# Four-layer block: weight loads moved behind the first expert unit, row one-hots on another engine, and a longer lead of the keys

## The chip, the core and the metric

The kernel runs on one core of a Trainium2 chip. The metric is the device time of one execution in microseconds (us); lower is better. A core has five engines that run their own instruction streams side by side and wait for one another through semaphores: TensorE (PE, matrix products and transpositions), VectorE (DVE), ScalarE (ACT), GpSimd (POOL) and SyncE (SP). SP issues most plain transfers, POOL issues the indirect ones (gathers of rows by an index), and ACT can issue plain transfers too. Each engine works strictly in the order of its own stream.

## What is computed

The input is 32 x 64 x 512 numbers, that is 2048 tokens of 512. Four layers are added to it one after the other, each a "cond" step and an "ffn" step:

```python
x = x + L0_ffn(L0_cond(x))   # per-sample 64x64 mixing; then attention and a
                             # mixture of 7 experts (top 2) with one shared expert
x = x + L1_ffn(L1_cond(x))   # per-sample 64x64 mixing; then 32 experts, top 4
x = x + L2_ffn(L2_cond(x))   # low-rank adapters; then a soft mixture of 16 experts
x = x + L3_ffn(L3_cond(x))   # attention over a paged cache, 8 heads, 4 key groups,
                             # window 256; then a linear layer with int8 weights
```

For layer 1 the router takes the four largest of 32 logits for each token; each token's row goes through its four experts, and the results are added with softmax weights. In layer 3, keys and queries are normalised and rotated per head, the new keys and values are written over the cached ones, and each query attends to the last 256 positions:

```python
q, k, v = x @ Wq.T, x @ Wk.T, x @ Wv.T
q, k = rope(rms(q), pos), rope(rms(k), pos)
k_blocks = k_blocks.at[blk, :, off, :].set(k)      # v likewise
p = softmax(where(in_window, q @ k_all.T * scale, -inf))
out = (p @ v_all) @ Wo.T
```

## The kernel before, in words

Tokens lie in 16 tiles of 128 (NT = 16). The kernel is written in a tile framework: the source says what is done, and a scheduler puts the instructions of each engine in order and inserts the waits. `keep_in_program_order`, `g.pin` and `later=True` hold single instructions to the order of the source. Pools with a number of buffers (`bufs`) decide how far a producer can run ahead.

**Expert layers (class `Moe`).** Tokens are marked in groups of tiles. `put` turns the chosen experts of a group into slots: it makes one-hots over experts, counts with two matmuls (L778, L779) and gets, for each token and choice, a slot number. `mark` then writes token numbers into slots by a matmul of two one-hots: `b_` says which of 128 rows a slot is (L744, 128 wide), `a_` says which tile of slots (L744, 40 tiles wide in layer 1), and ScalarE scales `a_` by the token number (L750). TensorE multiplies them (L752) and VectorE adds the result to `tokens` (L753). Both `a_` and `b_` have one buffer. In layer 1 the groups are `{3: 4, 7: 4, 11: 4, 13: 2, 14: 1, 15: 1}`: three groups of four tiles (n = 4), one of two, two of one. When the last group is marked, `tokens` is copied to the integer `stok` (L792), and by it POOL gathers the rows of the first five slot tiles (`rows_of`, tile `xr`, issued at L284).

Before a tile of layer 1 can be routed, its rows of layer 0's experts are gathered (`yk`) and added to the stream by VectorE (L1010); TensorE applies the per-sample mixing (`mm`, L1094), ScalarE copies it (`c`, L1096), TensorE transposes (`tp`, L1100), ScalarE copies (`cT`, L1102), TensorE multiplies with the router (`rp`, L1105), and VectorE adds the bias (`lg`, L1107) and takes the largest values.

The experts themselves run in units of 320 slots (`run`). Five transposed tiles (`tp`, L924, copied to `xT`) make two units; `into` multiplies with gate and up weights (`gu`, L943), `out_of` with the down weights (`y`, L962). A layer-0 expert has 640 slots (two units), a layer-1 expert 320 (one unit). Weights come as one transfer of 1.5 MB for each expert into a pool of three buffers (`weights`, tile `wt`, issued by SP at L213); the first two are fetched before the experts start, and `run`, which both layers share, asks for the others:

```python
for e in range(3):
    if (u * UNIT // C + e) < E:
        self.weights(u * UNIT // C + e) if u >= 1 or e < 2 else None
```

With `u = 0` the third is not asked for, so the source asks for it in the second unit. It needs nothing but a free buffer, and SP's stream has it early: it is issued at 411.24 us in layer 0, beside the gathers of the first rows, and at 721.83 in layer 1. Beside layer 0's experts, a generator prepares layer 3: it loads constants (`cst3`, `kvlen`, the block table) and the int8 layer's weights `w_i8` (1 MB), computes block numbers on VectorE, and much later reduces `w_i8` to scales (`wsc`).

**Layer 3.** Projections go unit by unit: `kv_i` (keys and values of tile i) and `q_i` alternate, with the queries `LAG` tiles behind (`units`). A unit is four matmuls (`pp`, L1870). For a unit, ScalarE squares (`sq`, L1965), VectorE sums (`ss`), POOL takes the power (`r`, L1970), VectorE normalises (`n`), POOL and VectorE multiply with the rotation tables (`ts` on POOL, `tc` on VectorE, L1988), and VectorE adds (`qkv`, L1997). For keys the tile is written to `newkv`; for queries `heads` transposes it (L1844) into `qT`. Queries from tile `NT - LAG` on are "late": they are copied to `qlate`, and rotated beside the attention by the generator `queries`. The last three tiles' queries (`LAST = 3`) are projected by `project` (L1928) inside the attention loop, at `s = -3, -2, -1`. When all keys are written, POOL gathers the new rows over the cached ones (`new_rows`, tile `kvt`, 96 gathers, L284); the attention loop runs over 64 half-samples: `keys` transposes (`kp`, L2021; copied to `kT`, L2025), `scores` (`sp`, L2048; softmax at L2055 to L2062), `turn` transposes the probabilities (`pT`, L2070), `values` (`op`, L2095), then the output projection (`y`, L2117).

Of the kernel before, what the change touches and what calls it, by code (L numbers as in the profile page):

```python
# [14 lines left out]
AF = mybir.ActivationFunctionType  # L15
ALU = mybir.AluOpType
# [4 lines left out]
P = 128  # L21
B, T, D = 32, 64, 512
NT = B * T // P
# [7 lines left out]
UNIT = 320  # L31
# [367 lines left out]
class Front:  # L399
# [43 lines left out]
    def weights(self, i):  # L443

        self.asked = self.g.cond_weights(self.sb, "wc0", self.at, i) if i < NT else None
# [235 lines left out]
class Moe:  # L681
# [25 lines left out]
        self.wp = ctx.enter_context(tc.tile_pool(name=f"ew{E}", bufs=3, reuse_waits="tile"))  # L707
        self.wts, self.bds = {}, {}

    def weights(self, e):  # L710
        if e < self.E and e not in self.wts:
            t = self.wp.tile([P, self.wlen], F32, name="wt")
            self.g.dma(t, self.g.a[self.wname][e * P : (e + 1) * P, :])
            self.wts[e] = t
        return self.wts.get(e)

# [13 lines left out]
    def mark(self, sb, ps, tok, sl, slot, ov, i, n, tiles):  # L730


        nc, iota, K = self.g.nc, self.g.c("iota"), self.K
        ai = sb.tile([P, n, K], I32, name=f"ai{n}")
        nc.vector.tensor_single_scalar(ai, slot, 7, ALU.arith_shift_right)
        tl = sb.tile([P, n, K], F32, name=f"tl{n}")
        nc.vector.tensor_copy(tl, ai)
        row = sb.tile([P, n, K], F32, name=f"row{n}")
        nc.vector.scalar_tensor_tensor(row, tl, -float(P), sl, ALU.mult, ALU.add)
        nc.vector.tensor_tensor(tl, tl, ov, ALU.add)  # L740
        a_ = sb.tile([P, n * K, tiles], F16, name=f"a_{n}", bufs=1)
        b_ = sb.tile([P, n * K, P], F16, name=f"b_{n}", bufs=1)
        for o, w, v in ((a_, tiles, tl), (b_, P, row)):
            nc.vector.tensor_tensor(  # L744
                o, iota[:, 0:w].unsqueeze(1).to_broadcast([P, n * K, w]),
                v.rearrange("p n k -> p (n k)").unsqueeze(2).to_broadcast([P, n * K, w]), ALU.is_equal,
            )
        for j in range(n):
            aj = a_[:, j * K : (j + 1) * K, :]
            nc.scalar.activation(aj, aj, AF.Copy, scale=self.g.c("tok")[:, i + j : i + j + 1])  # L750
        for k in range(n * K):
            nc.tensor.matmul(ps, b_[:, k, :], a_[:, k, :], start=k == 0, stop=k == n * K - 1)  # L752
        nc.vector.tensor_tensor(tok, tok, ps, ALU.add)  # L753
# [156 lines left out]
    def run(self, xs, per_tile):  # L910

        g, nc, tc, E, K, C = self.g, self.g.nc, self.g.tc, self.E, self.K, self.C
        units = E * C // UNIT
        with ExitStack() as ctx:
            sb = ctx.enter_context(tc.tile_pool(name=f"es{E}", bufs=3, reuse_waits="tile"))
            ps = ctx.enter_context(tc.tile_pool(name=f"eps{E}", bufs=2, space=PSUM, reuse_waits="tile"))
            xrs, xTs, hTs = self.xrs, {}, {}

            def turn(p):
                xT = sb.tile([P, 4, 2 * UNIT], F32, name="xT", bufs=2)  # L920
                for j in range(5):
                    tp = ps.tile([P, 4, P], F32, name="tp", tag="tp")
                    for c in range(4):
                        nc.tensor.transpose(tp[:, c, :], xrs[5 * p + j][:, c * P : (c + 1) * P], g.ident)  # L924
                    out = xT[:, :, j * P : (j + 1) * P]
                    if self.scale is None:
                        g.evac(out, tp)
                    else:
                        nc.vector.tensor_tensor(
                            out, tp, self.scale.unsqueeze(2).to_broadcast([P, 4, P]), ALU.mult  # L930
                        )
                xTs[p] = xT

            def into(u):
                wg, wu, _, bias = self.parts(self.weights(u * UNIT // C))
                xT = xTs[u // 2][:, :, (u % 2) * UNIT : (u % 2 + 1) * UNIT]
                hT = sb.tile([P, 2, UNIT], F32, name="hT", bufs=3)
                for ic in range(2):
                    gu = []
                    for wj in (wg, wu):  # L940
                        o = ps.tile([P, UNIT], F32, name="gu", tag="gu", bufs=4)
                        for c in range(4):
                            nc.tensor.matmul(  # L943
                                o, wj[:, c, ic * P : (ic + 1) * P], xT[:, c, :], start=c == 0, stop=c == 3
                            )
                        gu.append(o)
                    self.act(g, sb, hT[:, ic, :], *gu, None if bias is None else bias[:, ic::2])
                hTs[u] = hT

            def out_of(t):  # L950
                y = ps.tile([P, D], F32, name="y", tag="y")
                p, j = t // 5, t % 5

                pieces = {
                    0: [(0, 0, 0, P)], 1: [(0, P, 0, P)], 2: [(0, 2 * P, 0, 64), (1, 0, 64, 64)],
                    3: [(1, 64, 0, P)], 4: [(1, 64 + P, 0, P)],
                }[j]
                for ic in range(2):
                    for u, col, row, n in pieces:
                        u += 2 * p  # L960
                        wd = self.parts(self.weights(u * UNIT // C))[2]
                        nc.tensor.matmul(  # L962
                            y[row : row + n, :], hTs[u][:, ic, col : col + n], wd[:, ic, :],
                            start=ic == 0, stop=ic == 1,
                        )
                yo = sb.tile([P, D], F32, name="yo", bufs=4)
                if self.bias:
                    for u, col, row, n in pieces:
                        r = slice(row, row + n)
                        bd = self.bds[(u + 2 * p) * UNIT // C]  # L970
                        nc.vector.tensor_tensor(yo[r], y[r], bd[r], ALU.add)  # L971
                else:
                    g.evac(yo, y)
                nc.sync.dma_start(out=self.ys[t * P : (t + 1) * P, :], in_=yo)
                per_tile(sb, ps, t)

            pairs = units // 2
            turn(0)
            for u in range(units):
                p = u // 2  # L980
                if u % 2 == 0 and p + 1 < pairs:
                    self.rows_of(p + 1)
                for e in range(3):
                    if (u * UNIT // C + e) < E:
                        self.weights(u * UNIT // C + e) if u >= 1 or e < 2 else None
                into(u)
                self.bias_of(u * UNIT // C)

                if u % 2 == 0 and p > 0:
                    for j in (2, 3, 4):  # L990
                        out_of(5 * (p - 1) + j)
                if u % 2 == 1:
                    out_of(5 * p)
                    out_of(5 * p + 1)
                    if p + 1 < pairs:
                        turn(p + 1)
            for j in (2, 3, 4):
                out_of(5 * (pairs - 1) + j)
            if isinstance(per_tile, Side):
                per_tile.finish()  # L1000
# [577 lines left out]
def layer3_ahead(g, pool, w):  # L1578
# [15 lines left out]
    nc.sync.dma_start(out=ki, in_=a["kvlen"].rearrange("o b -> b o"))  # L1594
    tab = sb.tile([B, NBLK], I32, name="tabi")
    nc.sync.dma_start(out=tab, in_=a["table"])
    wt = g.load(sb, "w_i8")
    yield

    w["ridx"] = ridx = sb.tile([P, NT], I32, name="ridx")  # L1600
# [29 lines left out]
    nc.vector.tensor_scalar(slots[:, 0:KB], iota[0:B, 0:KB], s0p, None, ALU.add)  # L1630
    nc.vector.tensor_scalar(slots[:, KB:], iota[0:B, 0:5], wsp, None, ALU.add)
    blk = sb.tile([B, KB + 5], F32, name="blk")
    yield
    for j in range(KB + 5):
        hot = sb.tile([B, NBLK], F32, name="hot3", bufs=2)
# [44 lines left out]
    later = []  # L1680
# [85 lines left out]
            yield  # L1766


LAG = 5
LAST = 3  # L1770


def layer3(g, w, xs, xb):
# [3 lines left out]
    with ExitStack() as ctx:  # L1777
# [36 lines left out]
        with ExitStack() as c1:  # L1814
# [38 lines left out]
            for u in range(len(units) + 5):  # L1853
# [10 lines left out]
                if u < len(units):  # L1864
# [4 lines left out]
                    for c in range(4):  # L1869
                        nc.tensor.matmul(  # L1870
                            pp, xT[i][:, c, :], (w["w_kv3"] if z else wq)[:, c, :], start=c == 0, stop=c == 3
                        )
                    late = not z and i >= NT - LAG
                    out = wp.tile([P, D], F32, name=f"qlate{i}") if late else sb.tile([P, D], F32, name="qkv3", bufs=6)
                    outs.append(out)
                    if late:
# [60 lines left out]
        for s in range(-3, last + 8):  # L1937
            if s == -3:
                project(NT - LAST)
            if s % 2 == 0:  # L1940

                if s >= 4:
                    for _ in range(3):
                        old_rows()
                new_rows(s // 2 + 4)
            elif s == -3:
                new_rows(2)
            for stage, at in (("keys", s + 3), ("turn0", s), ("scores", s + 2), ("turn1", s)):
                if 0 <= at <= last:
                    getattr(f, stage)(at)  # L1950
            if -3 < s < LAST - 3:
                project(NT - LAST + s + 3)
            f.out()
            if s >= 2 and s % 2 == 0:
                next(beside, None)
            if 0 <= s - 1 <= last:
                f.values(s - 1)
# [222 lines left out]
```

## Time and profile before

| | |
|---|---|
| runs | 2704.36, 2704.14, 2700.83 us; median 2704.14 |
| the profiled execution | 2703.36 us, span 2701.6 us |
| mean granted TensorE clock | 0.97 |
| busy, share of the span | PE 93%, DVE 52%, ACT 27%, POOL 32% |
| DMA | 343.58 MB in the span, mean 127 GB/s |

Where things happen in the trace of before (us from the start of the span):

| stretch | what |
|---|---|
| 0 to 410 | layer 0: mixing, attention, shared expert, routing |
| 410 to 633 | layer 0's experts |
| 633 to 745 | layer 1's mixing and routing |
| 745 to 1231 | layer 1's experts |
| 1231 to 2279 | layer 2 |
| 2279 to 2392 | layer 3's projections |
| 2392 to 2701 | layer 3's attention and the int8 layer |

How to read the lines: a timeline row has its start, its duration, the engine, the line of the kernel, the operation, the tile written and the tiles read, shapes, the number of instructions that were put together, and in brackets the time for which the engine stood idle just before it and what ended that. A row of busy time by stretch has the stretch, its length, the busy time of PE, PEld (weight loads), DVE, ACT and POOL with the number of instructions, then the granted clock (1.00 is full), the DMA engines' busy share and GB/s. A matmul's end is modelled, so a row of several matmuls is better read by its starts.

### The profile page before, as it was taken

The numbers are of one execution on the slowest core, as the hardware profiler recorded it, in microseconds if no ns is written. First come the engines' busy times: TensorE is split into PE (matmuls) and PEld (weight loads), VectorE is DVE, ScalarE is ACT, GpSimd is POOL, SyncE is SP. The second block draws the span as 40 slices with busy tenths as digits, with TensorE's granted clock in tenths as the row PEclk, the third lists the DMA queues.
The fourth block names the chain that finished last, engine by engine and source line by source line (L and its number), as shares of the span: only waits on it lengthen the run. The fifth ranks groups of instructions, "written<-read, shape, count | busy, mean of one in ns | idle before, by whom it ended". The sixth has DMA issues, their size and how long they took to land.

```text
span 2701.6 us, 42326 instructions
## 1 busy us (share of the span) xinstructions
PE 2524.0 (93%) x16508; PEld 1620.7 (60%) x16523; DVE 1417.6 (52%) x3439; ACT 725.6 (27%) x1503; POOL 852.3 (32%) x904
## 2 busy tenths in 40 slices
PE   7999998996699999996999999999999999979998
PEld 5777775563565555564666666666666665435554
DVE  4666655643744444443544445555544431647886
ACT  2444430111311121110222222222222221236664
POOL 2222214623232233213233333333233321563440
PEclk9999989997699999998999999999999999989999
DMA  2333214445656976544122222222222223423441
GB/s 98 131 126 117 88 67 169 161 147 184 222 184 219 343 256 212 209 173 176 52 73 73 81 80 72 72 72 72 72 75 70 92 63 117 158 77 111 135 136 48
DMA packets 136213, 343.58 MB, mean 127 GB/s; under 512 B 24249, under 2 KB 25049, under 8 KB 128704
## 3 DMA queue, kind: packets, MB, share of 16 engines
q1 hardware_dynamic: 100368, 245.84, 26.3%
q0 software_dynamic: 35056, 89.13, 10.9%
q10 hardware_dynamic: 576, 5.77, 0.5%
q8 instruction: 134, 2.20, 0.3%
q14 instruction: 79, 0.65, 0.1%
HBM read 247.10 MB, written 109.58 MB: 132 GB/s over the span
## 4 chain that ended last, share of the span: by engine, by line
PE 41%; DVE 9%; issue 2%; DMA 1%; ACT 1%; POOL 0%; another core or an unknown queue 0%; SPq 0%; ACTq 0%; POOLq 0%; DVEq 0%
PE out L1557 8%; PE lp L1414 7%; PE pp L1870 3%; PE gp L1546 3%; PE zp L1491 3%; PE yp L1359 2%; PE y L2117 2%; PE hp L1523 2%; PE op L2095 2%; PE pT L2070 2%; PE sp L2048 2%; DVE xt L1025 1%; PE ep L1500 1%; DVE inv L1450 1%; PE kp L2021 1%
## 5 line engine op out<-in xcount | busy, mean ns | idle before, releaser
L943 PE MATMUL gu<-xT,wt 128*128 128x320 f32 x1472 | 408.5, 434 | 0.0
L943 PEld LDWEIGHTS gu<-xT,wt 128*128 128x128 f32 x1472 | 278.7, 191 | 123.4 <-issue 16.4
L1557 PE MATMUL out<-sb_w,gT 128*128 128x512 f32 x512 | 233.5, 599 | 10.7 <-DVE nn L1394 6.6
L962 PE MATMUL y<-wt,hT 128*128 128x512 f32 (+1 forms) x552 | 240.2, 608 | 0.2 <-DVE yo L971 0.2
L1414 PEld LDWEIGHTS lp<-xnT,sb_mu 128*128 128x128 f32 x2048 | 234.8, 193 | 9.2 <-issue 6.7
L1414 PE MATMUL lp<-xnT,sb_mu 128*128 128x128 f32 x2048 | 237.8, 276 | 2.1 <-ACT xnT L254 1.3
L1491 PE MATMUL zp<-sb_w,xnT 128*128 128x512 f32 x512 | 228.6, 595 | 5.1 <-DVE z L1493 5.1
L284 POOL DMA_INDIRECT kvst<-kv,gidx x96 | 97.7, 1017 | 271.6 <-DMA oldkv<-kvst 197.5
L1550 DVE COPY gT<-gp 128x512 f32<-128x512 f32 x64 | 44.3, 692 | 248.8 <-PE gp L1546 248.4
L1557 PEld LDWEIGHTS out<-sb_w,gT 128*128 128x128 f32 x512 | 93.3, 190 | 115.7 <-issue 95.2
L1491 PEld LDWEIGHTS zp<-sb_w,xnT 128*128 128x128 f32 x512 | 93.7, 190 | 113.2 <-issue 100.0
L284 POOL DMA_INDIRECT xr<-rows,stok x115 | 110.3, 959 | 153.3 <-PE tp L924 81.8
L284 POOL DMA_INDIRECT kvt<-newkv,oidx x96 | 97.8, 1019 | 135.6 <-DMA kvt<-oldkv 70.8
L962 PEld LDWEIGHTS y<-wt,hT 128*128 128x128 f32 (+1 forms) x552 | 80.5, 172 | 98.5 <-issue 83.2
L677 POOL TENSOR_TENSOR ga<-ga,sg 128x320 f32<-128x320 f32 x64 | 55.2, 862 | 266.2 <-ACT sg L673 262.7
L284 POOL DMA_INDIRECT yk<-ys,slot x96 | 98.3, 1024 | 128.6 <-SPq L823 66.2
L1528 ACT ACTIVATE h<-hp 128x512 f32<-128x512 f32 x128 | 69.5, 594 | 217.0 <-PE hp L1523 216.8
L673 ACT ACTIVATE sg<-ga 128x320 f32<-128x320 f32 x64 | 30.0, 469 | 278.5 <-DVE ga L671 274.7
L924 PEld LDWEIGHTS tp<-sb_cst,xr 128*128 128x128 f32 x460 | 54.8, 149 | 67.4 <-issue 38.4
L1419 DVE TENSOR_TENSOR lT<-lp,cmu 128x512 f32<-128x512 f32 x64 | 43.5, 680 | 94.5 <-PE lp L1414 93.6
L971 DVE TENSOR_TENSOR yo<-y,bd 128x512 f32<-128x512 f32 (+1 forms) x96 | 66.3, 691 | 50.1 <-PE y L962 46.4
L2055 DVE CUSTOM_DVE_ANT_0 s<-sp,mask 128x336 f32<-128x336 f32 x128 | 60.8, 503 | 59.8 <-PE sp L2048 25.1
(380 smaller groups left out, 4565.0 us busy)
## 6 DMA issues: line engine op xcount, KB each, us to landing
wt<-w_e SPq DMA_DIRECT2D x32, 1538.0 KB
ys<-yo SPq DMA_DIRECT2D x115, 256.0 KB
oldkv<-kvst SPq DMA_DIRECT2D x96, 224.0 KB
kvt<-oldkv SPq DMA_DIRECT2D x96, 224.0 KB
ys<-zero SPq DMA_DIRECT2D x10, 2048.0 KB
xt<-x SPq DMA_DIRECT2D x62, 256.0 KB
x<-xt SPq DMA_DIRECT2D x48, 256.0 KB
wt<-w_e SPq DMA_DIRECT2D x7, 1536.0 KB
```

The lines of the kernel that those rows point to most:

```text
L284: ins = self.nc.gpsimd.indirect_dma_start(out=out, out_offset=None, in_=src, in_offset=bass.IndirectOffsetOnAxis(ap=idx, axis=0), **kw)
L677: nc.gpsimd.tensor_tensor(ga, ga, sg, ALU.mult)
L943: nc.tensor.matmul(o, wj[:, c, ic * P : (ic + 1) * P], xT[:, c, :], start=c == 0, stop=c == 3)
L962: nc.tensor.matmul(y[row : row + n, :], hTs[u][:, ic, col : col + n], wd[:, ic, :], start=ic == 0, stop=ic == 1,)
L971: nc.vector.tensor_tensor(yo[r], y[r], bd[r], ALU.add)
L1414: g.first(e + c, nc.tensor.matmul(lp[:, e, :], w["mu"][:, c, (4 * q + e) * P : (4 * q + e + 1) * P], self.xnT[:, c, :], start=c == 0, stop ...
L1491: g.first(c, nc.tensor.matmul(zp, self.xnT[:, c, :], w["w1"][:, c, cols], start=c == 0, stop=c == 3))
L1528: g.pin(nc.scalar.activation(self.hs[q][b], hp[:, b], AF.Gelu))
L1546: g.first(e + b + k, nc.tensor.matmul(gp[r, e, cols], self.hs[q][b][:, e, r], self.lT[q][:, e, cols], start=True, stop=True))
L1557: g.first(e, nc.tensor.matmul(self.out, self.gTs[q][:, e, :], w["w2"][:, 4 * q + e, :], start=q + e == 0, stop=q + e == 6 and q == 3))
L1870: nc.tensor.matmul(pp, xT[i][:, c, :], (w["w_kv3"] if z else wq)[:, c, :], start=c == 0, stop=c == 3)
L2055: nc.vector.tensor_tensor_reduce(p, sps[j], self.masks[2 * i + half], -0.0625, 3.0e38, ALU.add, ALU.min, m)
```

## The change

It has three parts.

1. `weights` takes an engine that issues the transfer. In `run`, the third expert's weights are asked for right after the first unit's `into`, from ScalarE's queue; this holds for layer 0 and layer 1, which share the code. The load of `w_i8` goes two steps further down in the generator that prepares layer 3, and is held to the order of the source there.
2. In `mark`, for groups of four tiles (layer 1's first three groups, twelve tiles), `row` gets the opposite sign, and ScalarE makes `b_`: 16 times the absolute value of (column number minus row) over 128 columns, then one Relu of (1 minus that) over all 2048. `a_` stays on VectorE, and so do `a_` and `b_` of the smaller groups.
3. In layer 3, `LAG` is 8 (was 5), so the queries run eight tiles behind the keys and values; a new `LATE = 5` keeps the same five queries late. `project` makes tiles 13 and 14 at `s = -3` and tile 15 at `s = -2`. The transposed inputs have `LAG + 3` buffers, so 11 (was 8).

```diff
-    def weights(self, e):
+    def weights(self, e, eng=None):
         if e < self.E and e not in self.wts:
             t = self.wp.tile([P, self.wlen], F32, name="wt")
-            self.g.dma(t, self.g.a[self.wname][e * P : (e + 1) * P, :])
+            self.g.dma(t, self.g.a[self.wname][e * P : (e + 1) * P, :], eng)
...
-        nc.vector.scalar_tensor_tensor(row, tl, -float(P), sl, ALU.mult, ALU.add)
+        wide = n == 4
+        sign = -1.0 if wide else 1.0
+        nc.vector.scalar_tensor_tensor(
+            row, tl, -sign * P, sl, ALU.mult, ALU.subtract if wide else ALU.add
+        )
...
-        for o, w, v in ((a_, tiles, tl), (b_, P, row)):
+        if wide:
+            for k in range(n * K):
+                nc.scalar.activation(
+                    b_[:, k, :], iota[:, 0:P], AF.Abs, bias=row.rearrange("p n k -> p (n k)")[:, k : k + 1]
+                )
+            nc.scalar.activation(b_, b_, AF.Relu, bias=self.g.c("ones")[:, 0:1], scale=-1.0)
+        for o, w, v in ((a_, tiles, tl),) if wide else ((a_, tiles, tl), (b_, P, row)):
...
                 for e in range(3):
-                    if (u * UNIT // C + e) < E:
-                        self.weights(u * UNIT // C + e) if u >= 1 or e < 2 else None
+                    self.weights(u * UNIT // C + e) if u >= 1 or e < 2 else None
                 into(u)
+                if u == 0:
+                    self.weights(2, nc.scalar)
...
-    wt = g.load(sb, "w_i8")
     yield
...
     blk = sb.tile([B, KB + 5], F32, name="blk")
+    wt = g.load(sb, "w_i8", later=True)
     yield
...
-LAG = 5
+LAG = 8
+LATE = 5
...
-                    late = not z and i >= NT - LAG
+                    late = not z and i >= NT - LATE
...
             if s == -3:
                 project(NT - LAST)
+                project(NT - LAST + 1)
...
-            if -3 < s < LAST - 3:
-                project(NT - LAST + s + 3)
+            if -3 < s < LAST - 4:
+                project(NT - LAST + s + 4)
```

The scheduler's order after the change, beside the edits themselves: on ScalarE the copies `c` and `cT` of tiles 13, 14 and 15 come after the third group's Abs and Relu (the second group's stand ahead of tile 12's `cT`); on TensorE `mm` of tile 15 comes after tile 13's `rp`; on VectorE tile 15's first `L1010` comes ahead of the second group's `row`; on POOL the first gathers of `kvt` are mixed with `r` and `ts` of queries 7 to 12.

## The prediction

> **What bounds the kernel now.** I read the page's engine table, then the busy time by stretch, then the timelines of the three stages that the change edits.
>
> ```profile
> PE 2524.0 (93%) x16508; PEld 1620.7 (60%) x16523; DVE 1417.6 (52%) x3439; ACT 725.6 (27%) x1503; POOL 852.3 (32%) x904
> ...
> 416.00:418.00 2.00, 0.52 (x3) 0.52 (x4) 0.00 (x0) 0.00 (x0) 1.42 (x2) 0.50 0.96 377
> ...
> 720.00:730.00 10.00, 6.59 (x42) 5.47 (x42) 8.37 (x35) 4.73 (x8) 0.00 (x0) 0.50 0.92 351
> 730.00:740.00 10.00, 1.48 (x11) 1.24 (x12) 3.94 (x20) 1.34 (x4) 2.84 (x3) 0.50 0.64 210
> ...
> 2420.00:2425.00 5.00, 0.24 (x2) 0.00 (x0) 0.01 (x1) 0.59 (x1) 3.91 (x4) 0.50 0.13 31
> ```
>
> TensorE is busy 93% of the span, so an edit counts only where TensorE waits. Each edit aims at one such hole: layer 0's first expert tiles (412 to 425, DMA share 0.96), layer 1's routing (686 to 745), and the start of layer 3's attention (2392 to 2432). The 0.50 is the granted clock.
>
> **A: third expert's and int8 weights later.** The timeline of TensorE:
>
> ```profile
> 412.70 0.63 PE L924 MATMUL tp<-sb_cst,xr 128*128 128x128 f32 x4 [2.47 <-DMA xr<-rows,stok]
> 417.48 1.11 PE L924 MATMUL tp<-sb_cst,xr 128*128 128x128 f32 x4 [4.15 <-DMA xr<-rows,stok]
> 421.22 1.09 PE L924 MATMUL tp<-sb_cst,xr 128*128 128x128 f32 x4 [2.62 <-DMA xr<-rows,stok]
> ...
> 425.30 7.03 PE L943 MATMUL gu<-xT,wt 128*128 128x320 f32 x25
> ```
>
> TensorE waits for gathered rows. GpSimd issues a gather every 1.25 us from 409.16; the first is usable 2.5 us after its issue ended (410.21 to 412.70). The fifth is issued at 414.27 to 415.22, so with free DMA engines it is usable at 417.7; a transposition (1.1) and the DVE copy (0.68) make 419.5 the start of full work, against 425.30: 5.8 us. Two transfers go from this stretch: 1.5 MB of expert 2 (SP, 411.24) and 1 MB of w_i8 (SP, 418.17), 2.5 of some 5 MB that move at 350 to 400 GB/s. The 0.48 MB of constants stays, so I take **-5**; ends: -6.5, and -1 if the gathers' own pace sets the waits. The moved loads are hidden: expert 2 is used in the fifth unit (about 480), 50 us after its new place behind the second sigmoid (431 to 436); w_i8 is first read by a DVE reduction that moves with it. Uncovered, the expert load would cost 1.5 MB at 390 GB/s, 4 us. On ScalarE's queue only an issue of 0.3 to 0.4 us (SP's rows) stands ahead of the next sigmoid.
>
> The same lines move layer 1's third expert behind its second sigmoid (755.00 now), with waits for earlier gathers and GpSimd; the next sigmoid stands behind it. First use is the third unit's matmul at 771.19, 16 us on, against 4 us of load and 3.3 us for five gathers of 0.26 MB: nothing. Layer 1's first gather is issued at 736.41, when today's loads are mostly in: nothing gained.
>
> The Trainium skill (DMA: Bandwidth & Descriptors, "Issuing engines are not separate DMA queues") says that transfers from all engines share the same DMA engines, so another queue only saves issue time. By it, A pays for the delay of the load, not for ScalarE's queue, and a load issued at once on ScalarE would gain nothing; no row here separates the two.
>
> **B: row one-hots on ScalarE.** DVE loses three comparisons of 2.28 us (L744, 128x2048). ScalarE gets, for each of three groups of four tiles, 16 Abs of 128 columns and a Relu of 2048. Its L750 rows with an operand per partition cost 348 ns at 70 columns and 551 at 320, so 395 at 128; four of 320 in 1.92 us are spaced 0.457, 0.094 less than one lasts. An Abs then adds 0.30, sixteen 4.8; the Relu, on the same line, 1.95. With the four scalings (0.46 ahead, 1.4 behind) a group's train is 8.6 us. Ends: 0.16 an Abs (from the 64-column Exp, 257 ns) and a 1.06 Relu (L542, 1024 columns) give 5.5; 0.457 and 2.1 give 11.3.
>
> The place matters more than the sum. ScalarE runs in order, and what stands behind the trains is this:
>
> ```profile
> 704.60 0.17 DVE L739 SCALAR_TENSOR_TENSOR row<-tl,sl 128x16 f32<-128x16 f32 x1
> 704.89 2.28 DVE L744 TENSOR_TENSOR b<-sb_cst,row 128x2048 f16<-128x2048 f32 x1
> 706.10 0.59 ACT L1096 COPY c<-mm 128x512 f32<-128x512 f32 x1 [0.22 <-PE mm L1094]
> 717.26 2.02 PE L1094 MATMUL mm<-xt,wbd 128*128 128x512 f32 x2
> 723.76 0.19 DVE L1107 TENSOR_TENSOR lg<-rp,bc_b_r 128x32 f32<-128x32 f32 x1 [1.23 <-PE rp L1105]
> 734.73 0.43 PE L752 MATMUL tok<-a,b 128*128 128x80 f16 x4 [3.05 <-ACT a L750]
> ```
>
> In the changed order the copies c and cT of tiles 13, 14 and 15 come after group 3's train, and TensorE's mm of tile 15 comes after tile 13's router matmul. DVE has tile 15's first gathered addition ahead of group 2's row: today DVE waits until 703.93 for a gather issued at 697.78; the one needed is issued 1.45 us later, so it lands at about 705.3 and the row is ready at 705.7, no earlier than today's 704.60. Then: train 2 to 714.3; group 3 reuses the one buffer, so it starts when TensorE has read it (1.25), 715.6; train 3 to 724.2; c 0.59, tp 1.1, cT 0.59, rp 1.9, and latencies: mm of tile 15 at about 728.9 against 717.26, 11.6 us late. From there the chain to the last token matmul is today's, except that group 3's marking is already done, some 1.5 us. I take **+10**. Ends: row at 702.3 (all 2.28 saved), trains of 5.5 and full clock give -3; trains of 11.3 give +17.
>
> The clock enters this. The rows 720 to 740 ran at 0.50, though the longest idle stretch that TensorE shows between 708.9 and 730 is 1.97 us; I keep half clock. At full clock the matmuls on the way (tp 1.1 and rp 1.9 of tile 13; mm 2.02, tp 1.12 and rp 1.92 of tile 15) would halve, 4 us less, and B would be +6. The Trainium skill (TensorE: Matmul & The Clock Gate, "HAM oscillation") warns of idle gaps over some 3.4 us. If shorter gaps left the clock full, that +6 would be the term; the rows speak against it.
>
> **C: keys lead by eight tiles.** Three query projections leave the front of the last key projection, 3.87 us each (3.43 and 0.44): it ends 11.6 us earlier, and the first gather of new rows comes at 2382.2 instead of 2393.82. TensorE's total work is unchanged.
>
> ```profile
> 2393.82 1.22 POOL L284 DMA_INDIRECT kvt<-newkv,oidx  x1 [0.85 <-DMA xt<-x2b]
> 2425.32 0.98 POOL L284 DMA_INDIRECT kvt<-newkv,oidx  x1 [0.30 <-issue]
> ...
> 2394.53 0.63 PE L1844 MATMUL tp<-sb_cst,qkv 128*128 128x128 f32 x4 [2.25 <-DVE qkv L1997]
> 2425.73 0.82 PE L2021 MATMUL kp<-sb_cst,kvt 112*128 112x112 f32 x3 [5.50 <-ACT kT L2025]
> 2431.34 1.47 PE L2095 MATMUL op<-pTs,kvt 112*64 112x128 f32 x12
> ```
>
> The 24 gathers take 1.285 us each. Only after the last (2426.3) do the late copies go through, and the first values matmul comes 5.0 us later. In the changed order the gathers are mixed with the rotations of the queries still to come (r 1.64, ts 1.28), one queue. So GpSimd's work is conserved: from 2382.2 it has only some 4.8 us of idle time today (2.1, 1.77, 0.85), and its train can end at 2421.5, not 11.6 earlier. The rotations, waiting behind gathers, also delay the transpositions of queries 7 to 10, which stand ahead of project(13) in TensorE's order: the one idle of 2.25 becomes several, to about 2406. The gap moves more than it closes: values at 2426.5 to 2431. I take **-3**; ends: -11.6, and +4 if the train ends as late as now and the late heads push the keys.
>
> **Sum.** The profiled execution took 2703.36 (span 2701.6 and 1.8 around it), 0.8 below the median of the runs. 2703.36 - 5 + 10 - 3 = 2705.4, on the median's footing 2706. About 0.2%, 5.4 us, is what a measurement of this kernel can tell from no change.
>
> **Rivals.**
> (1) Slower: ScalarE's train is dearer. With B at +17, -5 + 17 - 3 = +9, 2713. It decides from B over 13.4, an Abs of more than 0.41 us in place of 0.30 (two trains on the path). For: 320 columns are spaced 0.457; against: the 70-column row.
> (2) Faster: the keys' lead pays in full. -5 - 11.6, with B at +6 from full clock: -10.6, 2693. For: TensorE idles 15 us in 2392 to 2428; against: one GpSimd queue.
> (3) A does not do what it says: gathers under their own load keep the pace, A is -1, sum +6, 2710. For: the gathers alone move 2.5 MB there; against: the DMA share of 0.96 with three other transfers.
>
> **Chances.** Forecast 0.48 (no change), rival 1 0.17 and rival 3 0.13 (slower, 0.30), rival 2 0.22 (faster). The range 2693 to 2714 takes in the rivals' centres and leaves out about half of rivals 1 and 2.
>
> **What would show it.** A: gu at full pace from 419 to 420. B: the first layer-1 gather at about 741 if A is taken off (736.41 now plus 10, less 5); c of tile 13 behind Abs and Relu. C: first kvt gather 11 to 12 us earlier against the last kv projection, heads gaps before project(13), values 0 to 5 earlier. Wrong: c of tile 13 not waiting for ScalarE, or the values 8 us earlier.

## The result and the profile after

The changed kernel takes 2711.52 us (median of 20 runs, 2703.76 to 2718.70) against 2700.93 for the kernel before (20 runs): ratio 1.0027, 95% interval [1.0018, 1.0037]: 7.3 us slower by that ratio, while the two medians stand 10.6 us apart (a second measurement, e12 below, gives 10.5). Either way the change makes the kernel slower. The forecast of 2706 (no change) missed by 5.5; the range 2693 to 2714 held it. The profiled execution of after took 2711.10, span 2709.3.

The same lines as before, from the page and from the busy time by stretch of after (line numbers behind the edits are 12 to 16 higher than in before):

```profile
PE 2528.1 (93%) x16508; PEld 1623.8 (60%) x16523; DVE 1412.3 (52%) x3436; ACT 743.6 (27%) x1554; POOL 852.1 (31%) x904
```

```profile
416.00:418.00 2.00, 2.00 (x9) 1.53 (x10) 1.03 (x4) 0.00 (x0) 1.39 (x3) 0.50 0.73 202
...
440.00:450.00 10.00, 7.48 (x28) 3.63 (x26) 8.46 (x28) 0.58 (x1) 4.64 (x5) 0.80 0.38 116
450.00:460.00 10.00, 10.00 (x36) 6.99 (x35) 2.16 (x4) 0.87 (x2) 5.88 (x10) 0.86 0.27 79
720.00:730.00 10.00, 4.68 (x30) 3.91 (x30) 0.55 (x4) 8.63 (x19) 0.00 (x0) 0.50 0.14 52
```

The hole at 416 is closed, as A meant; a new one is open at 440 to 460: TensorE stands for 2.5 of ten us and then runs at a lower clock. In before it was busy throughout at full clock there, and VectorE was full beside it:

```profile
430.00:440.00 10.00, 10.00 (x39) 7.05 (x38) 10.00 (x57) 0.87 (x2) 4.01 (x6) 1.00 0.15 51
440.00:450.00 10.00, 10.00 (x41) 5.32 (x40) 10.00 (x32) 1.61 (x3) 2.87 (x3) 1.00 0.21 61
```

At 720 to 730 ScalarE is what is busy in after.

**A in the timeline of TensorE:**

```profile
412.71 0.63 PE L936 MATMUL tp<-sb_cst,xr 128*128 128x128 f32 x4 [2.50 <-DMA xr<-rows,stok]
414.68 0.66 PE L936 MATMUL tp<-sb_cst,xr 128*128 128x128 f32 x4 [1.34 <-DMA xr<-rows,stok]
...
420.64 18.11 PE L955 MATMUL gu<-xT,wt 128*128 128x320 f32 x62
438.58 3.60 PE L974 MATMUL y<-wt,hT 128*128 128x512 f32 x8
...
442.98 1.07 PE L974 MATMUL y<-wt,hT 128*64 128x512 f32 x2
446.57 1.97 PE L936 MATMUL tp<-sb_cst,xr 128*128 128x128 f32 x8 [2.52 <-DVE xT L941]
448.47 1.98 PE L974 MATMUL y<-wt,hT 128*64 128x512 f32 x4
...
451.29 9.56 PE L955 MATMUL gu<-xT,wt 128*128 128x320 f32 x32
```

The rows arrive sooner and `gu` runs at 420.64 instead of 425.30. But the lead melts: 5.6 us at the very first `gu` (417.73 against 423.38), 4.7 at this row, 3.5 at the first `y` (438.58 against 442.13; the `gu` of after run at half clock until 422), and 0.2 at the third unit's `gu` (451.29 against 451.53). In the last step TensorE stood 2.52 us for a copy `xT`, and the transpositions behind it take 1.97 where eight take 1.04 at full clock. VectorE at that time:

```profile
429.20 0.49 DVE L663 SCALAR_TENSOR_TENSOR sg<-gu,sg 128x320 f32<-128x320 f32 x1 [5.29 <-issue]
...
430.75 0.53 DVE L1650 SCALAR_TENSOR_TENSOR hot<-sb_cst,slots,tabf 32x257 f32<-32x257 f32 x1
...
443.37 0.47 DVE L1650 SCALAR_TENSOR_TENSOR hot<-sb_cst,slots,tabf 32x257 f32<-32x257 f32 x1
...
445.83 1.28 DVE L941 TENSOR_TENSOR xT<-tp,sb_ln 128x512 f32<-128x512 f32 x2
```

Between the first and the last `hot` lie 26 look-ups of layer 3's preparation, spaced 0.41 us. They stood in before too (431.58 to 444.82). Now TensorE comes 3.5 us earlier and the look-ups end only 1.0 earlier: VectorE stood 5.29 us ahead of `sg` first, for ScalarE's sigmoid of 428.73.

The look-ups are not the whole difference. In before the copies `xT` came late as well, 2.7 us behind the start of the transpositions (3.8 in after), and TensorE didn't wait for them:

```profile
442.13 3.60 PE L962 MATMUL y<-wt,hT 128*128 128x512 f32 x8
445.56 1.04 PE L924 MATMUL tp<-sb_cst,xr 128*128 128x128 f32 x8
446.53 2.99 PE L962 MATMUL y<-wt,hT 128*64 128x512 f32 x10
449.36 1.04 PE L924 MATMUL tp<-sb_cst,xr 128*128 128x128 f32 x8
...
451.53 8.78 PE L943 MATMUL gu<-xT,wt 128*128 128x320 f32 x32
```

```profile
448.26 1.27 DVE L929 TENSOR_TENSOR xT<-tp,sb_ln 128x512 f32<-128x512 f32 x2
```

Ten `y` matmuls stood between the first transpositions and the next ones (446.53 to 449.36) and covered the wait; in after there are two (442.98). So by these rows the stall takes late copies and TensorE's new order together.

**B in the timelines of ScalarE, TensorE and GpSimd:**

```profile
708.06 4.78 ACT L751 ACTIVATE b<-sb_cst,row 128x128 f16<-128x128 f32 x16 [1.78 <-DVE lg L1121]
...
713.19 1.99 ACT L754 ACTIVATE b<-b,sb_cst 128x2048 f16<-128x2048 f16 x1
...
718.03 4.78 ACT L751 ACTIVATE b<-sb_cst,row 128x128 f16<-128x128 f32 x16 [1.03 <-DVE row L742]
...
726.42 1.04 ACT L1110 COPY c<-mm 128x512 f32<-128x512 f32 x2
...
730.55 2.06 PE L1108 MATMUL mm<-xt,wbd 128*128 128x512 f32 x2
...
749.54 0.94 POOL L284 DMA_INDIRECT xr<-rows,stok  x1 [45.83 <-DVE stok L804]
```

Sixteen Abs take 4.78 us (0.30 each), the Relu 1.99. The copies `c` of tiles 13 and 14 come at 726.42, when the third train is over, `mm` of tile 15 at 730.55 (717.26 in before), the first gather 13.1 later than in before (2.1 of this was there when the stage began: the last gather of layer 0's results is issued at 702.60 against 700.49).

**C in the timelines of GpSimd and TensorE:**

```profile
2393.71 1.39 POOL L284 DMA_INDIRECT kvt<-newkv,oidx  x1 [2.36 <-DMA kvt<-oldkv]
2395.13 1.67 POOL L1986 TENSOR_TENSOR r<-ss,sb_cst 128x8 f32<-128x8 f32 x1
...
2398.05 1.28 POOL L2004 TENSOR_TENSOR ts<-n,tab 128x512 f32<-128x512 f32 x1
...
2435.14 0.98 POOL L284 DMA_INDIRECT kvt<-newkv,oidx  x1 [0.31 <-issue]
...
2408.75 1.09 PE L1859 MATMUL tp<-sb_cst,qkv 128*128 128x128 f32 x4 [6.34 <-DVE qkv L2013]
2414.30 1.09 PE L1859 MATMUL tp<-sb_cst,qkv 128*128 128x128 f32 x4 [4.46 <-DVE qkv L2013]
2418.56 1.09 PE L1859 MATMUL tp<-sb_cst,qkv 128*128 128x128 f32 x4 [3.17 <-DVE qkv L2013]
```

Set against the first projection (11.2 us later than in before), the first gather is 11.3 us earlier, but the 24th only 1.4: `r` and `ts` stand between them. Three query transpositions wait 14 us for those products.

### The profile page after: what moved, and what is told of

Same layout as the page of the kernel before. It is cut to its first block, busy times and chain, and to the rows that moved or that the text cites. A ratio compares the mean times of both kernels' runs of the same rounds, so it can differ in the third digit from the quotient of the medians.

```text
span 2709.3 us, 42377 instructions
## 1 busy us (share of the span) xinstructions
PE 2528.1 (93%) x16508; PEld 1623.8 (60%) x16523; DVE 1412.3 (52%) x3436; ACT 743.6 (27%) x1554; POOL 852.1 (31%) x904
## 4 chain that ended last, share of the span: by engine, by line
PE 41%; DVE 10%; issue 1%; POOL 1%; DMA 1%; ACT 0%; SPq 0%; ACTq 0%; POOLq 0%; DVEq 0%
PE out L1571 8%; PE lp L1428 7%; PE gp L1560 3%; PE pp L1885 3%; PE zp L1505 3%; PE yp L1373 2%; PE y L2133 2%; PE hp L1537 2%; PE op L2111 2%; PE pT L2086 1%; PE sp L2064 1%; DVE xt L1039 1%; PE ep L1514 1%; DVE inv L1464 1%; DVE mx L1441 1%
## 5 line engine op out<-in xcount | busy, mean ns | idle before, releaser
L1571 PE MATMUL out<-sb_w,gT 128*128 128x512 f32 x512 | 233.5, 599 | 11.2 <-DVE nn L1408 6.6
L1466 POOL TENSOR_TENSOR eT<-eT,inv 128x512 f32<-128x512 f32 x64 | 71.8, 1122 | 57.9 <-DVE inv L1465 34.3
```

Of the source, the lines that this page charges most:

```text
L1466: g.pin(nc.gpsimd.tensor_tensor(e3, e3, inv.unsqueeze(2).to_broadcast([P, 8, T]), ALU.mult))
L1571: g.first(e, nc.tensor.matmul(self.out, self.gTs[q][:, e, :], w["w2"][:, 4 * q + e, :], start=q + e == 0, stop=q + e == 6 and q == 3))
```

## How the runs are compared

One profiled execution differs from the next by some us in places that no edit touches. So I set beside the times the length of the stage that an edit touches, from starts of instructions in each run's trace: **A start** from layer 0's slot numbers (`stok`) to the first `gu`, **A stage** from the same slot numbers to the first gather of layer 1, so that it contains A start; **B** from the last gather of layer 0's results to layer 1's `stok`; **C** from the first projection to the first values matmul, and to the end of the program.

| kernel | time to before, us [95%] | A start | A stage | B | C values | C end |
|---|---|---|---|---|---|---|
| before | 0 | 15.2 | 234.1 | 35.0 | 150.5 | 417.3 |
| after | +7.3 [4.9, 10.0] | 9.6 | 237.2 | 46.0 | 146.5 | 413.8 |
| e1 A | +1.3 [-2.7, 5.4] | 11.6 | 236.4 | 34.5 | 147.4 | 416.5 |
| e2 B | +10.2 [5.7, 14.6] | 15.3 | 233.3 | 46.3 | 148.1 | 415.1 |
| e3 C | -5.7 [-10.0, -1.3] | 14.7 | 234.4 | 33.6 | 146.6 | 411.9 |
| e4 A held | -4.9 [-8.9, -0.8] | 11.3 | 232.0 | 34.5 | 148.4 | 415.2 |
| e9 pieces | -15.4 [-19.2, -11.6] | 14.6 | 227.9 | 33.6 | 150.5 | 419.7 |
| e10 A held, pieces | -20.8 [-25.4, -16.2] | 11.4 | 226.7 | 33.9 | 148.3 | 417.9 |
| e11 after, held | +4.1 [0.8, 7.3] | 9.8 | 232.0 | 46.0 | 146.3 | 414.3 |
| e12 after again | +10.5 [6.8, 14.3] | 10.2 | 234.0 | 46.2 | 146.8 | 414.1 |
| e5 C, ts moved | +2.9 [0.0, 5.8] | 15.2 | 233.0 | 34.5 | 144.5 | 404.7 |
| e6 B, two groups | +2.4 [-0.5, 5.3] | 15.4 | 232.6 | 40.0 | 141.3 | 403.6 |
| e7 third expert alone | +1.9 [-0.8, 4.5] | 10.3 | 232.4 | 34.4 | 141.5 | 405.2 |
| e8 A held, C | +1.3 [-1.9, 4.2] | 10.3 | 231.0 | 33.8 | 146.9 | 406.7 |

The second column is the ratio's distance from 1 times the median of before, measured beside it on the same chip. In the table "held" means that VectorE's look-ups are held back, and "pieces" that the 64-row matmuls stand together; both are explained below. The last four ran on another chip, where before itself takes 2656 us (2696 to 2703 on the others); their stages are compared with each other. Each row's stages come from one trace; those of kernels that share a stage unedited differ by 1.4 to 4.6 us (the most for C's end).

Theory after the first reading: B and C cost what was forecast; A's gain at the start is real, and is lost again because VectorE is behind with the look-ups. Rival: the parts disturb one another, or the moved loads themselves land late.

## The experiments

**The parts alone.** e1 is before with the edits of A, e2 with those of B, e3 with those of C.

> Part A alone (third expert's weights and w_i8 later), B and C as before. Theory (backlog): the first gu comes 5.7 us earlier than before, but VectorE's 26 block look-ups (0.41 us each, 10.6 us) still end at about 444, so the copies of the second pair's xT come late, TensorE stands 2.5 us and falls to half clock; from the third unit on the experts are 3 to 4 us late: +3.5 us, ratio 1.0013. Rival (the loss comes only together with B or C): -5 us, ratio 0.998, third unit's gu 5 us earlier than before.

> Part B alone (row one-hots of three groups on ScalarE). Theory (place): c and cT of tiles 13 to 15 stand behind the third group's train; last router logits 11 us later than before, layer 1's first gather 10 us later, nothing regained: +10 us, ratio 1.0037. Rival (part of the delay came from A's late weights or from its later start): +6 us or less.

> Part C alone (keys and values lead by eight tiles). Theory: the first gather of new rows comes 11.3 us earlier, the 24th only 1 to 2 us earlier since GpSimd's queue is shared with the rotations, the first values matmul 3 to 4 us earlier: -3.5 us, ratio 0.9987. Rival (the lead pays in full when it is alone): -11 us, ratio 0.996.

B and C alone give what they give together: +11.3 and -3.9 in their own stages against before. A alone, too, starts sooner (11.6) and ends its stage later (236.4). The trace of e1 has the same hole, 2.5 us ahead of `tp` at 450.05, with the clock at 0.50 at 452 to 455. Its whole time, +1.3 [-2.7, 5.4], shows neither a gain nor a loss, but leaves out the rival's -5. By the stages the parts don't disturb one another. C alone gained no more up to the first values than with the others; its rival fell.

**A with the look-ups held.** The first of each four look-ups is kept behind what stands ahead of it in the source, and the generator hands over after four instead of eight:

```diff
-        nc.vector.scalar_tensor_tensor(
+        g.first(j % 4, nc.vector.scalar_tensor_tensor(
             hot, iota[0:B, 0:NBLK], slots[:, j : j + 1], tabf, ALU.is_equal, ALU.mult,
             accum_out=blk[:, j : j + 1],
-        )
-        if j % 8 == 7:
+        ))
+        if j % 4 == 3:
             yield
```

> Part A alone, but VectorE's 26 block look-ups are held to the order of the source (first of each four), so that they stand behind the second pair's xT copies. Theory (backlog): xT is not late, no idle stretch and no half clock at 444 to 460; the gain at the start stays: -3 to -5 us, ratio 0.9982 to 0.9989. Rival (the loss after 440 comes from the moved weights or the changed order of the y matmuls): still +2 to +3.5 us, ratio 1.001.

> The changed kernel whole, with VectorE's look-ups held to the order of the source. Theory (backlog): no idle stretch behind the second pair's transpositions, 5 to 6 us faster than the changed kernel in the same call; ratio to before 1.0007 if the changed kernel is at 1.0027. Rival (A's loss comes back elsewhere once B and C are there): as the changed kernel.

> The changed kernel as it is, beside the run with the look-ups held. Theory: 1.0027 again where layer 2 takes 1015 us; where it takes 989 us (as in the runs of the last call) the first values matmul of layer 3 no longer waits for the last gather in before, so part C is a loss of 2 us and not a gain of 3: 1.0045. Rival (C's gain doesn't depend on that): 1.0027 in both.

The timeline of TensorE in e11, where `y` starts at 438.58 as it does in after:

```profile
438.58 3.60 PE L974 MATMUL y<-wt,hT 128*128 128x512 f32 x8
442.01 1.04 PE L936 MATMUL tp<-sb_cst,xr 128*128 128x128 f32 x8
442.98 1.07 PE L974 MATMUL y<-wt,hT 128*64 128x512 f32 x2
443.98 1.09 PE L936 MATMUL tp<-sb_cst,xr 128*128 128x128 f32 x8
445.00 1.08 PE L974 MATMUL y<-wt,hT 128*64 128x512 f32 x4
...
446.50 8.78 PE L955 MATMUL gu<-xT,wt 128*128 128x320 f32 x32
455.21 4.70 PE L974 MATMUL y<-wt,hT 128*64 128x512 f32 x10
```

No wait, and `gu` 7.92 us behind `y` instead of 12.71: 4.8 us; the unit's 32 `gu` then take 8.71 instead of 9.49, since the clock is full: 0.8 more, together 5.6. The look-ups now start at 458.85. TensorE's order here is that of after, with two `y` between the transpositions, and the same loads move in both kernels: neither is enough for the stall without the backlog. Whether before's order of TensorE would have covered it no run shows.

Holding the look-ups makes the whole change 6.8 us faster beside the unheld one (2706.19 against 2712.99) and A alone 5.2 (2692.86 against 2698.10). It doesn't take back all of A's loss. From the first `gu` to layer 1's first gather, before takes 218.9 us (234.1 less 15.2), after 227.6, e11 222.2: of 8.7 us lost, 5.4 come back, and 3.3 stay. The longer half clock at the start and the lost pairs of 64-row matmuls, told below, are about 1 us each; the rest is open.

e12 ran on a chip where layer 2 takes 1015 us, so theory and rival both said 1.0027; it gave 1.0039 [1.0025, 1.0053] and doesn't separate them. Its traced execution, 2706.92, was the fastest of its six (the others 2711 to 2715); TensorE stood only 1.12 us there, the clock stayed full, and the stage is 234.0, as in before. So the same kernel has the hole in one execution and hardly in another.

**Which load.** e7 moves the third expert's weights alone.

> Of part A only the third expert's weights move, w_i8 keeps its place. Theory: two thirds of the gain at the start stay (from the slot numbers to the first expert matmul 12 us, 15 without A, 10.8 with A), and VectorE's backlog stays in full (7 to 9 us more from the first expert matmul to the 200th): +3 to +5 us, ratio 1.0015. Rival (w_i8's move pulls the look-ups ahead): no backlog, -3 us, ratio 0.999.

The start takes 10.3 us, as with both loads on this chip (e8): the expert's weights are the whole gain, and `w_i8`, issued at 418.17 behind the gathers that matter, gives nothing there. So 10.3 and not 12. The other half missed too: from the first `gu` to the 200th it takes 95.8 us, 3.4 more than the 92.2 to 92.6 of the kernels without A on this chip, where 7 to 9 were expected, and the stage (232.4) is level with theirs (232.6 and 233.0). One thing that differs is ScalarE's first sigmoid, which was not late: 425.51, where the eighth `gu` ends at 425.47 by the trace; in after it ends at 423.17 and the sigmoid starts at 428.73.

```profile
425.51 0.44 ACT L662 ACTIVATE sg<-gu 128x320 f32<-128x320 f32 x1 [15.50 <-PE gu L943]
```

```profile
428.73 0.44 ACT L662 ACTIVATE sg<-gu 128x320 f32<-128x320 f32 x1 [21.12 <-PE gu L955]
```

**B with two groups** (`wide = n == 4 and i < 8`).

> Part B alone, for the first two groups of four tiles only; the third group's row one-hots stay on VectorE. Theory (place: the trains of groups 2 and 3 stand one after the other before the copies of tiles 13 to 15): one train of 8.4 us leaves the path, so from the last gather of layer 0's results to the last router logits it takes 27 us (22 to 23 without B, 35.5 with B): +4 us, ratio 1.0015. Rival (each group costs its third): 31 us, +7 us, ratio 1.0026.

Up to the last logits it takes 28.6 us, nearer to 27 than to 31; the stage is 40.0 against 34.2 without B and 46.1 with all three groups, 5.8 us more, which lies between the theory's 4 and the rival's 7. One train of the three carries half of the cost: place counts, but the second train has its price too (in e6 it ends at 707 and the next `cT` waits for it).

**C without `ts` in the train.** For queries behind the last key projection, `ts` goes to VectorE.

> Part C alone, and the sine products (ts) of the queries behind the last key projection on VectorE instead of GpSimd; nothing is left out. Theory (one GpSimd queue): with C the four ts of 1.27 us and the gaps at them, some 5.7 us, stand in the gather train; without them the 24th gather comes 5 us earlier (137 to 138 us from the first projection, 142.7 with C alone), TensorE's three waits for rotated queries (14 us together) shrink to under 8, the first values matmul comes 4 us earlier, and the time is -8 to -10 us, ratio 0.9965. Rival (TensorE and VectorE are held by something else while gathers are issued): the train ends at most 1 us earlier, time as with C alone, ratio 0.998.

The train did what was expected: the 24th gather comes 137.2 us from the first projection, 5.5 sooner than in e8 (142.7), and the wait for rotated queries is down to 3.8. But the values came only 2.4 sooner, and the time, +2.9 [0.0, 5.8], is no gain at all. A new wait took the place, on TensorE and behind it on VectorE:

```profile
2359.43 0.63 PE L1845 MATMUL tp<-sb_cst,qkv 128*128 128x128 f32 x4 [3.79 <-DVE qkv L2000]
...
2381.47 1.49 PE L2051 MATMUL sp<-kT,qT 64*128 64x336 f32 x2 [6.60 <-DVE m L2058]
```

```profile
2378.59 1.68 POOL L1973 TENSOR_TENSOR r<-ss,sb_cst 128x8 f32<-128x8 f32 x1
```

```profile
2380.30 0.69 DVE L1970 TENSOR_REDUCE ss<-sq 128x8 f32<-128x512 f32 x1 [9.28 <-POOL r L1973]
2380.91 0.50 DVE L2058 CUSTOM_DVE_ANT_0 s<-sp,mask 128x336 f32<-128x336 f32 x1
```

The `ss` of a late query waits 9.28 us for an `r` in GpSimd's train, and the first softmax stands behind it on VectorE. It is still GpSimd's queue, by another product. The train's share of the theory holds, the time doesn't.

**A held and C together.**

> Part A with VectorE's look-ups held to the order of the source, and part C; B left as before. Theory (the parts add): -2.7 from A as held and -2 to -5.7 from C: -5 to -8 us, ratio 0.997 to 0.998. Rival (A's gain is used up in later waits): as C alone.

This fell. On this chip the kernels without C have their first values at 141.3 and 141.5 us, before the 24th gather (143.9 and 144.1), and C has them at 146.9. So by the stages C is a loss of 5.5 there, 2.3 by the end, where it gained 2.3 and 3.4 on the other chips. That is one trace with C against two without; the whole time, +1.3 [-1.9, 4.2], is no gain, and C alone was not run there.

**The 64-row pieces.** Two units share a tile whose halves of 64 rows are separate matmuls. A changes TensorE's order there: in layer 0, 18 pairs of them start together in after and 20 in before. That led to e9, in which they are pinned side by side (`if n == 64: g.pin(ins)`) and stand between two transpositions of the next pair (`out_of(mid)` inside `turn`, after `j == 1`).

> The kernel before, with one thing more and none of the three parts: in the expert layers the down products of the 64-row piece that two units share stand together on TensorE (u, u+1, u, u+1), between the second and the third transposition of the next pair. In the traces such matmuls start 0.007 us apart and take 0.47 together when neighbours (54 starts in before), and 0.48 each when not; some 38 more can be neighbours. Theory (both halves of the array at once): -12 to -18 us, ratio 0.9935 to 0.9955. Rival (VectorE's copies of xT set the pace there, and the time turns into a wait): -2 us or less.

> As the run before it (neighbouring 64-row pieces), with part A and its look-ups held to the order of the source; B and C as before the change. Theory (the two add): -15 to -22 us, ratio 0.992 to 0.9945, 3 to 5 us under the run with the pieces alone. Rival (the gain of A as held is used up in a later wait): as the pieces alone.

In before, and in e9:

```profile
797.45 1.07 PE L962 MATMUL y<-wt,hT 128*64 128x512 f32 x2
798.45 1.09 PE L924 MATMUL tp<-sb_cst,xr 128*128 128x128 f32 x8
799.48 1.08 PE L962 MATMUL y<-wt,hT 128*64 128x512 f32 x4
```

```profile
784.41 1.94 PE L964 MATMUL y<-wt,hT 128*64 128x512 f32 x8
```

Eight take 1.87 us together (to the next transposition at 786.28); in before six take about 2.0 in their two groups. 92 pairs now start together in the two layers, 54 did in before. Layer 0's stage is 5.6 us shorter (227.9 against 233.5), layer 1's experts 8.6 (462.1 against 470.7 from first to last `gu`): 14 of the 15.4. With A held the kernel takes 2683.39 against 2702.91, ratio 0.9923 [0.9906, 0.9940], 3.8 us under the pieces alone. It beats both kernels.

## Why the prediction was right in part and wrong in part

The sum was -5 + 10 - 3 = +2. By stages (means of the traces with and without a part; for A those with both loads moved, the held look-ups and the pinned pieces left out; for C to the end, the other chip left out), it was A +2.4, B +11.9, C -3.4: +10.9, against +7.3 and +10.5 in the two measurements. A's three traces lie 0.5 to 3.7 above the mean without A. The range held the time because it was wide: A's own ends, -6.5 and -1, didn't hold A.

**A, the term that failed.** Its first half stands: the start takes 10.5 us instead of 15.1, 4.5 less, where 5.8 was worked out and 5 taken; rival 3's reason, that gathers keep their own pace, fell. What failed is the step "the moved loads are hidden" as the end of the account. The loads were hidden; VectorE was not. An earlier start moves TensorE toward work on another engine that doesn't start earlier, and the row for it was there in before: VectorE busy 10.00 of 10 at 430 to 450. I had named no work that is late next. Two smaller parts I had not seen either. The earlier `gu` start at half clock: it is 0.50 up to 422 in after and up to 425 in before, so "full pace from 419 to 420" came only at 422, and the 62 `gu` from 420.64 take 1.1 us more (17.94 against 16.83 by their starts). And two pairs of 64-row pieces lost their neighbour in layer 0 (two starts of some 0.5 us).

**B.** Mechanism and order as worked out: row at 707.79 (705.7), train 8.4 to 8.5 us (8.6), `mm` of tile 15 at 730.55 (728.9), 11.9 net instead of 10. The clock stayed at 0.50. Rival 1's dear Abs (0.41) fell at 0.30.

**C.** Right in size (-3.4 for -3), in the mixed queue and in the waits ahead of the projection of tile 13. The train's end was sized wrong: worked out 4.8 us earlier (2421.5 against 2426.3), it came 1.4 earlier, and GpSimd still stood 2.36 us ahead of the first gather. So the gain at the first values, 2.3 on the mean, is only in part that of the train. I didn't foresee that the gain could be missing on another chip.

**The sum.** The forecast case, no change, did not come: the time is near that of rival 3 (2710) for a reason that is none of the rivals'.

On the clock, the trace goes further than the page cited: TensorE at 0.52 in 446 to 447 and 0.57 in 452 to 453 shows half clock after an idle stretch of 2.52 us, and e1 at 452 to 455 after one of the same length, while e12, with 1.12 us in the same place, stays at 1.00. The Trainium skill (TensorE: Matmul & The Clock Gate, "HAM oscillation") puts the limit at some 3.4 us; here half clock followed 2.5.

```profile
446.00:447.00 1.00, 0.43 (x2) 0.43 (x3) 1.00 (x2) 0.00 (x0) 0.41 (x1) 0.52 0.76 240
...
452.00:453.00 1.00, 1.00 (x4) 0.61 (x3) 0.22 (x1) 0.00 (x0) 0.97 (x2) 0.57 0.09 33
```

## What to carry to other kernels

When an edit lets the bound engine start earlier, look down the stream for the next engine that is full and does not start earlier: the gain ends there, and with the clock it can turn into a loss. Background work that a scheduler may place freely belongs behind the copies that the bound engine needs. In a mixed queue an early start of one train pays at most by the idle time of that queue.

## What the runs showed of the hardware that was not expected

- Matmuls that fill 64 columns each run side by side when they are neighbours: starts 0.007 us apart, 0.47 us for both, against 0.48 each alone. The Trainium skill (TensorE: Matmul & The Clock Gate, "Why this matters for your kernels") states it for small outputs in different column groups; the traces agree.
- ScalarE's first sigmoid starts 3.2 to 6.1 us after the trace's end of its matmuls in the six kernels with both loads moved on the first chips, while GpSimd issues gathers, and 0.04 us after it in all four on the other chip; in the four kernels on the first chips without these loads moved it is 0.1 to 1.3. Ends of matmuls are modelled, so whether the result or its signal is late stays open.
- The chips differ by 40 to 47 us in the kernel before. Layer 2, which no edit touches, takes 1015 to 1019 us from its first `lp` to layer 3's first projection on the first chips and 987 to 990 on the other. One VectorE row shows a part of it, the last maximum of a tile, in before and in e7:

```profile
L1431 DVE TENSOR_TENSOR mx<-mx x16: 291/1569/1699, 1285.1 to 2198.0; 128x128 f32<-128x128 f32 x16
```

```profile
L1433 DVE TENSOR_TENSOR mx<-mx x16: 291/292/341, 1274.2 to 2159.7; 128x128 f32<-128x128 f32 x16
```

In before it stands beside a GpSimd product (1369.83 to 1370.88, L1452); in e7 a later VectorE operation does (1358.76, L1442, beside a product of 1358.78) and takes 1.64 instead of 0.69. The Trainium skill (GPSIMD Engine Reference, "1. Specifications") says that VectorE with two SBUF inputs contends with GpSimd; that fits, but why the two meet at another operation on another chip was not tested.
